# Routed expert blocks advanced one stage at a time, with later constant tables, in a macaron layer on one core

## The chip, the core and the metric

One Trainium2 chip, one core of it. The metric is device time of the whole program in microseconds (us), lower is better; every run's time is that of one launch. The core's engines are named as in the profile: PE (TensorE, matrix products and transpositions), DVE (VectorE), ACT (ScalarE), POOL (GpSimd) and SP (SyncE, which here only issues transfers).

## The reference

x has 8 sequences of 256 tokens with 256 features, float32, so 2048 tokens. The layer is a "macaron": half a feed-forward block, attention, half a feed-forward block, each behind a layer norm.

```
x = x + 0.5 * ffn(layernorm(x))
x = x + attention(layernorm(x))
x = x + 0.5 * ffn(layernorm(x))

ffn(x):                                  # E = 8 experts, K = 2, H = 176
    scores = softmax(x @ gate_w)
    topk_w, topk_idx = top_k(scores, 2)
    routed = sum over the 2 chosen experts e of
             topk_w * ((silu(x @ w_gate[e]) * (x @ w_up[e])) @ w_down[e])
    shared = (silu(x @ sw_gate) * (x @ sw_up)) @ sw_down     # width 352
    return routed + shared

attention(x):                            # 16 heads of 128, one key/value head
    an index score I of 16 small heads picks, for every token, 32 earlier tokens;
    softmax attention over those, then @ wo
```

The gate of the experts is not computed for every expert and token: only the two chosen experts' rows matter, and the kernel uses that.

## The kernel before

Tokens lie in 16 tiles of 128 tokens by 256 features, and x stays in on-chip memory all the time. The function `ffn(n, ...)` is called twice, n = 0 ahead of the attention and n = 1 behind it. The order of instructions on each engine is not written out by hand: the Python code is traced, and a scheduler with priorities from the traced order makes one queue for each engine, each worked off in order. A wait in a queue therefore holds up all that stands behind it in that queue.

**Loads and layer norm.** x is loaded in groups of tiles, 0–1, 2–3, 4–7, 8–11 and 12–15 (L102 to L104), by SP's queue, behind it the shared expert's weights (L107 to L115). `expert_loads` (L121) are six loads of the experts' weights into `wall`, 704 KB each: two pairs of gate and up weights and a pair of down weights; `ffn` lets two of them be issued behind each of the first three groups' layer norms. `layernorm` (L214 to L256) works group by group: statistics `st` (L218) and `mv` (L219) on DVE, `ve` (L221), the square root on ACT, `rstd` (L226), then for each tile `xn` (L248, five buffers), its store to `xn_dram` by SP's queue (L252), its transposition `pt` on PE (L255) and the copy `xnT` on ACT (L256).

**Shared expert.** For each tile `pg` (L455) gives the gate of the shared expert and the router's logits; ACT takes `lg` (L462) and `sg`, the silu (L464). Later `pu` (L472) on PE, `gt` (L480) on DVE, three transpositions `ptg` (L491) on PE, copies `gT` (L492, L494), the product `po` (L498) and the addition to x on DVE (L503). These tiles' work is spread between the other stages.

**Routing.** `route` (L258 to L433) sorts the 4096 pairs of token and expert into blocks of 128 slots that each belong to one expert: 37 blocks (`ND`) are always worked, two more only if the counts ask for them (`rare`, L619). It uses two tables of counts, `place` (128 x 1024) and `block` (128 x 1248), that POOL makes with `iota` (L191, called from L649 and L650).

**Routed blocks.** For block b, POOL gathers its 128 rows from `xn_dram` into `xs` (`fetch`, L511; 8 + 2 buffers); PE transposes them (`px`, L522), ACT copies to `xsT` (L524); PE multiplies with the expert's gate and up weights (`pgu`, L534, `widen`), whose place is read from a table into a register of PE (`locate`); ACT takes the silu `sl` (L544), DVE multiplies to `h` (L546); PE transposes h (`ph`, L562, `turn_hidden`), DVE copies to `hT` (L564); PE multiplies with the down weights (`py`, L570, `narrow`); DVE makes the weight `ws` from two columns that came with the gathered row (L578); ACT scales to `y` (L587) and POOL scatters y to `y_dram` (L589). `routed` (L600 to L616) calls these; its body is quoted here, since the order in it is what the diff rewrites:

```
for b in range(ND):
    h = widen(b)
    if b > 0:
        narrow(b - 1, slot_pool)
    if b + XB < ND:
        fetch(b + XB, slot_pool)
    if b + 2 < ND:
        turn(b + 2)
    turn_hidden(b, h)
narrow(ND - 1, slot_pool)
```

**Behind the loop.** The two result rows of each token are read back by plain transfers (`yg`, L634) and added on DVE (`combine`, L640). In the first call the attention stage follows, in the second the output's store.

Of the kernel before, what the change touches and what calls it, by code (L numbers as in the profile page):

```python
# [23 lines left out]
def macaron_kernel(  # L24
# [42 lines left out]
    SCALE = HD ** -0.5  # L67
    DR = D + 16
    XB = 8
    XH = 2  # L70
    SB = 8
    WAIT = 3
    YB = 1
# [24 lines left out]
    wk_sb = wts.tile([P, KD, HD], F32, name="wk_sb")  # L98
    wv_sb = wts.tile([P, KD, HD + HI], F32, name="wv_sb")

    starts = [0, 2, 4, 8, 12, NT]
    groups = [range(a, b) for a, b in zip(starts, starts[1:])]  # L102
    for g in groups:
        nc.sync.dma_start(out=x[:, g.start : g.stop, :], in_=xr[:, g.start : g.stop, :])  # L104
    nc.scalar.dma_start(out=wsg_sb[:, :, 0:HS], in_=sw_gate.rearrange("(k p) h -> p k h", p=P))
    nc.scalar.dma_start(out=wsg_sb[:, :, HS:], in_=gate_w.rearrange("(k p) e -> p k e", p=P))
# [79 lines left out]
    ones = const.tile([P, P], BF16, name="ones")  # L186
    nc.gpsimd.memset(ones, 1.0)

    def counted(name, pattern, base=0, channel=0, dtype=F32, pool=const):
        t = pool.tile([P] + [n for _, n in pattern], dtype, name=name, bufs=1)  # L190
        nc.gpsimd.iota(  # L191
            t, pattern, base=base, channel_multiplier=channel,
            allow_small_or_imprecise_dtypes=True,
        )
        return t

    expert8 = counted("expert8", [[0, NT], [1, E]], base=-E)
# [236 lines left out]

        return token, dest, choice, cols, used

    def ffn(n, pool, block_pool, behind):

# [2 lines left out]
        xn_dram = dram.tile([NT * P, DR], F32, name=f"xn_dram_{n}")  # L443
        y_dram = dram.tile([(2 * NT * K + NB) * P, D], F32, name=f"y_dram_{n}")
        lg = pool.tile([P, NT, E], F32, tag="lg", name=f"lg_{n}", bufs=1)
        sg = {}
        for tiles in groups:
            layernorm(tiles, xn_dram, table=(n == 0))
            for load in expert_loads[0:2]:
                load()  # L450
            del expert_loads[0:2]
            for i in tiles:
                pg = psum.tile([P, HS + E], F32, tag="A", name=f"pg_{n}_{i}")
                for k in range(KD):
                    nc.tensor.matmul(  # L455
                        pg,
                        xnT[:, k, i * P : (i + 1) * P],
                        wsg_sb[:, k, :],
                        start=(k == 0),
                        stop=(k == KD - 1),  # L460
                    )
                nc.scalar.copy(lg[:, i, :], pg[:, HS:])  # L462
                sg[i] = pool.tile([P, HS], F32, tag=f"sg{i}", name=f"sg_{n}_{i}", bufs=1)
                nc.scalar.activation(sg[i], pg[:, 0:HS], AF.Silu)  # L464

        gts = {}

# [35 lines left out]
            nc.vector.scalar_tensor_tensor(x[:, i, :], po, 0.5, x[:, i, :], ALU.mult, ALU.add)  # L503

        w = wall.rearrange("p e c -> p (e c)")
        xs, xsT, hT, c0 = {}, {}, {}, {}

        def fetch(b, slot_pool):

# [8 lines left out]
        def turn(b):  # L518

            px = psum.tile([P, KD, P], F32, tag="B", name=f"px_{n}_{b}")  # L520
            for k in range(KD):
                nc.tensor.transpose(px[:, k, :], xs[b][:, k * P : (k + 1) * P], ident)  # L522
            xsT[b] = block_pool.tile([P, KD, P], F32, tag="xsT", name=f"xsT_{n}_{b}", bufs=3)
            nc.scalar.copy(xsT[b], px)  # L524

        def locate(b):
# [3 lines left out]
        def widen(b):  # L530

            pgu = psum.tile([P, 2, HE], F32, tag="A", name=f"pgu_{n}_{b}")
            for k in range(KD):
                nc.tensor.matmul(  # L534
                    pgu,
                    xsT[b][:, k, :],
                    w[:, bass.ds(c0[b] + 2 * k * HE, 2 * HE)],
                    start=(k == 0),
                    stop=(k == KD - 1),
                )  # L540
            if b + 1 < ND:
                locate(b + 1)
            sl = block_pool.tile([P, HE], F32, tag="sl", name=f"sl_{n}_{b}", bufs=3)
            nc.scalar.activation(sl, pgu[:, 0, :], AF.Silu)  # L544
            h = block_pool.tile([P, HE], F32, tag="h", name=f"h_{n}_{b}", bufs=3)
            scaled = nc.vector.tensor_tensor(h, sl, pgu[:, 1, :], ALU.mult)  # L546
            if attn_loads:
                load = attn_loads.pop(0)()
                tc.add_manual_dep(
                    load.ins,  # L550
                    scaled.ins.name,
                    mybir.DependencyInfo(
                        mybir.DependencyClass.Sync, mybir.DependencyReason.DATA
                    ),
                    reason="spread over the blocks",
                )
            return h

        def turn_hidden(b, h):
            ph = psum.tile([HH, 2, P], F32, tag="C", name=f"ph_{n}_{b}")  # L560
            for c in range(2):
                nc.tensor.transpose(ph[:, c, :], h[:, c * HH : (c + 1) * HH], ident)  # L562
            hT[b] = block_pool.tile([HH, 2, P], F32, tag="hT", name=f"hT_{n}_{b}", bufs=3)
            nc.vector.tensor_copy(hT[b], ph)  # L564

        def narrow(b, slot_pool):

            py = psum.tile([P, D], F32, tag="D", name=f"py_{n}_{b}")
            for c in range(2):
                nc.tensor.matmul(  # L570
                    py,
                    hT[b][:, c, :],
                    w[0:HH, bass.ds(c0[b] + 2 * KD * HE + c * D, D)],
                    start=(c == 0),
                    stop=(c == 1),
                )
            ws = block_pool.tile([P, 1], F32, tag="ws", name=f"ws_{n}_{b}", bufs=4)
            nc.vector.scalar_tensor_tensor(  # L578
                ws,
                xs[b][:, D + 1 : D + 2],  # L580
                choice[:, b : b + 1],
                xs[b][:, D : D + 1],
                ALU.mult,
                ALU.add,
            )
            y = slot_pool.tile([P, D], F32, tag="y", name=f"y_{n}_{b}", bufs=SB)
            nc.scalar.mul(y, py, ws)  # L587

            stored = nc.gpsimd.indirect_dma_start(  # L589
                out=y_dram,  # L590
                out_offset=bass.IndirectOffsetOnAxis(ap=dest[:, b : b + 1], axis=0),
                in_=y,
                in_offset=None,
            ).ins
            tc.declare_no_dep(stored, group=f"y_{n}", reason="rows that differ")
            tc.add_to_no_dep_group(f"y_{n}", stored)

        def routed(slot_pool):


            for b in range(XB):
                fetch(b, slot_pool)
            locate(0)
            turn(0)
            turn(1)
            for b in range(ND):
                h = widen(b)
                if b > 0:
                    narrow(b - 1, slot_pool)
                if b + XB < ND:  # L610
                    fetch(b + XB, slot_pool)
                if b + 2 < ND:
                    turn(b + 2)
                turn_hidden(b, h)
            narrow(ND - 1, slot_pool)

        def rare(count, slot_pool):

# [25 lines left out]
        def meanwhile(count):  # L644
            for _ in range(count):
                shared(next(tiles))

        with tc.tile_pool(name=f"route{n}", bufs=1, reuse_waits="tile") as tables:
            place = counted(f"place_{n}", [[1, P], [0, NA * K]], dtype=BF16, pool=tables)  # L649
            block = counted(f"block_{n}", [[1, NB], [0, NT * K]], dtype=BF16, pool=tables)  # L650
            token, dest, choice, cols, used = route(n, lg, xn_dram, place, block, tables, pool, meanwhile)
        meanwhile(behind)
        count = nc.values_load(used[0:1, 0:1], min_val=0, max_val=NB)
        with tc.tile_pool(name=f"slots{n}", bufs=1, reuse_waits="tile") as slot_pool:
            routed(slot_pool)
# [222 lines left out]
    with (  # L878
        tc.tile_pool(name="blocks0", bufs=3) as block_pool,
        tc.tile_pool(name="ffn0", bufs=3) as pool,  # L880
    ):
        results, combine, shared, left = ffn(0, pool, block_pool, behind=2)
        for i in left:
            shared(i)

# [69 lines left out]
    with (  # L955
        tc.tile_pool(name="blocks1", bufs=3, reuse_waits="tile") as block_pool,
        tc.tile_pool(name="ffn1", bufs=3, reuse_waits="tile") as pool,
    ):
        results, combine, shared, left = ffn(1, pool, block_pool, behind=2)

        def store(tiles):
            span = slice(tiles[0], tiles[-1] + 1)
            nc.sync.dma_start(out=outr[:, span, :], in_=x[:, span, :])


        late = left[-3:]
        with tc.tile_pool(name="late", bufs=1, reuse_waits="tile") as late_pool:
            for i in left[:-3]:
                shared(i)
            pairs = [range(i, min(i + 2, late[0])) for i in range(0, late[0], 2)]  # L970
            ends = [range(late[0], late[2]), range(late[2], NT)]
            yg = {g: results(g, late_pool, 7) for g in pairs[:4] + ends + pairs[4:]}
            for i in late:
                shared(i, first=lambda: [combine(g, yg[g]) for g in ends if g[0] == i])
                store([i])
            for g in pairs:
                combine(g, yg[g])
                store(g)
# [48 lines left out]
```

## Time and profile before

| | us |
|---|---|
| median of 7 runs | 974.93 (973.3 to 976.77) |
| time of the profiled execution | 974.67 |
| its span in the profile | 972.9 |
| PE busy | 943.5 (97%) |
| DVE busy | 582.6 (60%) |
| ACT busy | 418.5 (43%) |
| POOL busy | 291.1 (30%) |
| mean granted PE clock | 0.998 of full |

The span runs from the first to the last instruction of the profiled execution; the 1.8 us between it and that execution's time lie outside. The profile's page gives the busy time of each engine, and below it the costliest groups of instructions with the idle time ahead of them. Three further views are used below. The timeline lists an engine's instructions in order of start: start, duration, engine, line, operation, output and inputs, how many alike in a row, and in brackets the idle time ahead and what ended it. The waits add up idle time by the pair of what waited and what it waited for. The windows give, for a stretch of time, each engine's busy time, and at the end the granted clock of PE, the busy share of the DMA engines and GB/s. A matmul's duration in these rows is modelled and overlaps with the next one's: the distance from start to start is what it costs in a full queue.

### The profile page before, as it was taken

What the parts mean: (1) busy time and instruction counts of PE and PEld (TensorE: products, weight loads), DVE (VectorE), ACT (ScalarE), POOL (GpSimd) and SP (SyncE); (2) the same over time, 40 slices, a digit from 0 to 9 for tenths busy, and PEclk for the clock granted to TensorE, in tenths of its full rate; (3) what the DMA queues carried; (4) which work ended last, traced back from release to release, by engine and by line L of the source; (5) the groups of instructions that cost most, each with busy time, mean ns of one, the idle gap of its engine ahead of it and who ended that gap; (6) DMA issues with size and microseconds to landing.
All of it is one profiled execution on the core that took longest, in us unless ns stands there. A gap on an engine that the chain in (4) does not pass through costs nothing. (4 is left out here: it accounts for less than half of the span.)

```text
span 972.9 us, 15312 instructions
## 1 busy us (share of the span) xinstructions
PE 943.5 (97%) x4476; PEld 749.7 (77%) x4476; DVE 582.6 (60%) x1642; ACT 418.5 (43%) x1233; POOL 291.1 (30%) x333
## 2 busy tenths in 40 slices
PE   6999999999999999999999999999999989899997
PEld 3677776898888888888888888888877766677765
DVE  5453334986856756766765775585685554633336
ACT  4424443345544535545445444534444434144431
POOL 2037773001312212122221222222133320277740
PEclk9999999999999999999999999999999999999999
DMA  9316632420322222222222222322324330133317
GB/s 307 95 56 191 205 106 93 141 77 22 120 76 87 80 94 67 93 98 77 76 91 96 86 91 74 97 88 75 100 90 132 126 124 24 33 108 107 107 62 264
DMA packets 99576, 100.53 MB, mean 103 GB/s; under 512 B 15942, under 2 KB 82470, under 8 KB 99494
## 3 DMA queue, kind: packets, MB, share of 16 engines
q1 hardware_dynamic: 82502, 51.89, 17.9%
q0 software_dynamic: 14272, 45.18, 13.3%
q10 hardware_dynamic: 2720, 2.47, 0.9%
q8 instruction: 39, 0.64, 0.3%
q14 instruction: 43, 0.35, 0.1%
HBM read 58.07 MB, written 41.42 MB: 102 GB/s over the span
## 5 line engine op out<-in xcount | busy, mean ns | idle before, releaser
L815 POOL TENSOR_TENSOR s<-s,rden 128x512 f32<-128x512 f32 x64 | 93.8, 1466 | 233.0 <-DVE rden L814 128.9
L805 ACT ACTIVATE s<-s,anm 128x128 f32<-128x128 f32 (+1 forms) x256 | 113.0, 443 | 98.4 <-DVE anm L802 49.0
L869 PEld LDWEIGHTS pwo<-wo_sb,oT 128*128 128x128 f32 x512 | 96.4, 190 | 29.6 <-issue 12.0
L869 PE MATMUL pwo<-wo_sb,oT 128*128 128x256 f32 x512 | 117.3, 381 | 0.2 <-ACT oT L848 0.2
L749 DVE SCALAR_TENSOR_TENSOR index<-r,v,index 128x128 f32<-128x128 f32 (+1 forms) x240 | 111.8, 490 | 8.9 <-ACT r L742 7.1
L671 PE MATMUL pqT<-xnT,wq_sb 128*128 128x256 f32 x512 | 116.2, 379 | 0.0
L511 POOL DMA_INDIRECT xs<-xn_dram,token x74 | 71.6, 967 | 128.5 <-DVE dest L416 106.6
L671 PEld LDWEIGHTS pqT<-xnT,wq_sb 128*128 128x128 f32 x512 | 96.9, 190 | 12.4 <-issue 1.0
L671 PE MATMUL pqi<-xnT,wi_sb 128*128 128x224 f32 x512 | 102.8, 352 | 0.0
L534 PE MATMUL pgu<-wall,xsT 128*128 x296 | 100.3, 460 | 0.2 <-ACT xsT L524 0.2
L734 PE MATMUL pi<-kI,qi 128*128 128x128 f32 (+1 forms) x512 | 94.7, 334 | 3.6 <-ACT r L742 3.6
L671 PEld LDWEIGHTS pqi<-xnT,wi_sb 128*128 128x128 f32 x512 | 95.8, 190 | 1.0
L786 PE MATMUL ps<-kT,qT 128*128 128x256 f32 (+1 forms) x512 | 94.6, 327 | 1.7 <-DVE s L793 1.7
L822 DVE STREAM_TRANSPOSE sq<-s 128x512 f32<-128x512 f32 x64 | 62.3, 973 | 54.6 <-POOL s L815 54.6
L841 PE MATMUL pav<-s,v 128*128 128x512 f32 x192 | 93.0, 593 | 1.9 <-DMA s<-sq_dram 1.9
L786 PEld LDWEIGHTS ps<-kT,qT 128*128 128x128 f32 x512 | 81.2, 191 | 17.3 <-ACT r L742 5.1
L734 PEld LDWEIGHTS pi<-kI,qi 128*128 128x128 f32 x512 | 73.7, 191 | 21.0 <-ACT r L742 12.2
L793 DVE TENSOR_TENSOR s<-ps,mb 128x512 f32<-128x512 f32 x96 | 64.2, 681 | 36.8 <-PE ps L786 36.1
L589 POOL DMA_INDIRECT y_dram<-y,dest x74 | 72.2, 975 | 39.2 <-ACT xsT L524 17.5
L742 ACT ACTIVATE r<-pi 128x512 f32<-128x512 f32 x96 | 54.2, 589 | 66.9 <-DVE index L749 51.0
L570 PE MATMUL py<-wall,hT 88*128 x296 | 76.2, 379 | 0.0
L570 PEld LDWEIGHTS py<-wall,hT 88*128 88x128 f32 x296 | 55.9, 189 | 20.4 <-ACT y L587 1.1
(157 smaller groups left out, 1304.4 us busy)
## 6 DMA issues: line engine op xcount, KB each, us to landing
s<-sq_dram SPq DMA_DIRECT2D x384, 64.0 KB, 2.1
sq_dram<-sq POOLq DMA_DIRECT2D x32, 512.0 KB, 2.9
sq_dram<-sq POOLq DMA_DIRECT2D x32, 256.0 KB, 2.5
yg<-y_dram SPq DMA_DIRECT2D x18, 256.0 KB, 2.8
xn_dram<-xn SPq DMA_DIRECT2D x32, 128.0 KB, 1.8
yg<-y_dram SPq DMA_DIRECT2D x7, 512.0 KB, 7.3
wi_sb<-in_L_attn_wq_idx_dram SPq DMA_DIRECT2D x8, 256.0 KB, 3.6
wq_sb<-in_L_attn_wq_dram SPq DMA_DIRECT2D x8, 256.0 KB, 3.6
```

The lines of the kernel that those rows point to most:

```text
L511: nc.gpsimd.indirect_dma_start(out=xs[b], out_offset=None, in_=xn_dram, in_offset=bass.IndirectOffsetOnAxis(ap=token[:, b : b + 1], axis=0),)
L534: nc.tensor.matmul(pgu, xsT[b][:, k, :], w[:, bass.ds(c0[b] + 2 * k * HE, 2 * HE)], start=(k == 0), stop=(k == KD - 1),)
L570: nc.tensor.matmul(py, hT[b][:, c, :], w[0:HH, bass.ds(c0[b] + 2 * KD * HE + c * D, D)], start=(c == 0), stop=(c == 1),)
L589: stored = nc.gpsimd.indirect_dma_start(out=y_dram, out_offset=bass.IndirectOffsetOnAxis(ap=dest[:, b : b + 1], axis=0), in_=y, in_offset= ...
L671: nc.tensor.matmul(ps[:, j, :], weights(k, h0 + hh + j), xnT[:, k, b * S + skip : (b + 1) * S], start=(k == 0), stop=(k == KD - 1),)
L734: nc.tensor.matmul(pl[:, j, :], qi[:, hh + j, t * P : (t + 1) * P], kI[:, 0:ns], start=True, stop=True,)
L749: nc.vector.scalar_tensor_tensor(index[t], r[:, j, :], iw, index[t], ALU.mult, ALU.add)
L786: nc.tensor.matmul(ps[:, j, :], qT[:, j0 + j, t * P : (t + 1) * P], kT[:, 0:ns], start=True, stop=True,)
L805: nc.scalar.activation(s[:, j, :], s[:, j, :], AF.Exp, bias=nm[:, j : j + 1], scale=SCALE, accum_out=den[:, j : j + 1],)
L815: nc.gpsimd.tensor_tensor(s, s, rden.unsqueeze(2).to_broadcast([P, HG, ns]), ALU.mult)
L841: nc.tensor.matmul(po.rearrange("p q h k -> p (q h k)"), v[:, c, 0:HD], pT[:, c].rearrange("p q r -> p (q r)"), start=(c == 0), stop=(c == t),
L869: nc.tensor.matmul(po, oT[:, h, :], wo_sb[:, w0 + h, :], start=(h == 0), stop=(h == HW - 1),)
```

## The change

Four things change, all of them in or around `ffn`.

- The routed loop runs four steps longer and holds one stage of four different blocks in a step: the gate and up products of block b, the gathered rows' transposition of b + 2, the hidden layer's transposition of b − 2 and the down product of b − 4. `fetch` stands last in the step. `xsT`, `h` and `hT` get four buffers instead of three, `xs` thirteen instead of ten.
- `ws` is placed behind the copy `hT` of the same block in DVE's queue.
- In the first call the groups of tiles are 0, 1, 2–3, 4–7, 8–11, 12–15; in the second they stay as they were. The loads of x follow the first list. As two expert loads are issued behind each of the first three groups, they come behind the layer norms of tile 0, of tile 1 and of tiles 2–3.
- The iotas of `place` and `block` wait for the silu of tile 8 (`gate[NT // 2]`).

`behind` becomes the name of a helper that makes one instruction wait for another; what was the parameter `behind` is `ahead` now.

```diff
-    XH = 2
+    XH = 5
...
-    starts = [0, 2, 4, 8, 12, NT]
-    groups = [range(a, b) for a, b in zip(starts, starts[1:])]
-    for g in groups:
+    def grouped(*starts):
+        return [range(a, b) for a, b in zip(starts, (*starts[1:], NT))]
+
+    groups = [grouped(0, 1, 2, 4, 8, 12), grouped(0, 2, 4, 8, 12)]
+    for g in groups[0]:
         nc.sync.dma_start(out=x[:, g.start : g.stop, :], in_=xr[:, g.start : g.stop, :])
...
+    def behind(ins, other, reason):
+
+        tc.add_manual_dep(
+            ins.ins,
+            other.ins.name,
+            mybir.DependencyInfo(mybir.DependencyClass.Sync, mybir.DependencyReason.DATA),
+            reason=reason,
+        )
+
-    def counted(name, pattern, base=0, channel=0, dtype=F32, pool=const):
+    def counted(name, pattern, base=0, channel=0, dtype=F32, pool=const, after=None):
...
+        if after is not None:
+            behind(made, after, "not while VectorE is in a hurry")
...
-        for tiles in groups:
+        for tiles in groups[n]:
...
-                nc.scalar.activation(sg[i], pg[:, 0:HS], AF.Silu)
+                gate[i] = nc.scalar.activation(sg[i], pg[:, 0:HS], AF.Silu)
...
-            nc.vector.tensor_copy(hT[b], ph)
+            turned[b] = nc.vector.tensor_copy(hT[b], ph)
...
-            nc.vector.scalar_tensor_tensor(
-                ws,
...
+            with tc.issue_after(turned[b].ins):
+                nc.vector.scalar_tensor_tensor(
+                    ws,
...
-            for b in range(ND):
-                h = widen(b)
-                if b > 0:
-                    narrow(b - 1, slot_pool)
+            h = {}
+            for b in range(ND + 4):
+                if b < ND:
+                    h[b] = widen(b)
+                if b + 2 < ND:
+                    turn(b + 2)
+                if 2 <= b < ND + 2:
+                    turn_hidden(b - 2, h[b - 2])
+                if b >= 4:
+                    narrow(b - 4, slot_pool)
                 if b + XB < ND:
                     fetch(b + XB, slot_pool)
-                if b + 2 < ND:
-                    turn(b + 2)
-                turn_hidden(b, h)
-            narrow(ND - 1, slot_pool)
...
-            place = counted(f"place_{n}", [[1, P], [0, NA * K]], dtype=BF16, pool=tables)
-            block = counted(f"block_{n}", [[1, NB], [0, NT * K]], dtype=BF16, pool=tables)
+            late = dict(dtype=BF16, pool=tables, after=gate[NT // 2])
+            place = counted(f"place_{n}", [[1, P], [0, NA * K]], **late)
+            block = counted(f"block_{n}", [[1, NB], [0, NT * K]], **late)
```

More of the change, by code (lines that the diff above doesn't have):

```diff
@@ L187, in macaron_kernel @@
     nc.gpsimd.memset(ones, 1.0)
-    def counted(name, pattern, base=0, channel=0, dtype=F32, pool=const):
+    def behind(ins, other, reason):
[6 more added lines that the diff above has]
+    def counted(name, pattern, base=0, channel=0, dtype=F32, pool=const, after=None):
         t = pool.tile([P] + [n for _, n in pattern], dtype, name=name, bufs=1)
-        nc.gpsimd.iota(
+        made = nc.gpsimd.iota(
             t, pattern, base=base, channel_multiplier=channel,
@@ L435, in route, with ffn @@
         return token, dest, choice, cols, used
-    def ffn(n, pool, block_pool, behind):
+    def ffn(n, pool, block_pool, ahead):
         xn_dram = dram.tile([NT * P, DR], F32, name=f"xn_dram_{n}")
@@ L445, in ffn @@
         lg = pool.tile([P, NT, E], F32, tag="lg", name=f"lg_{n}", bufs=1)
-        sg = {}
-        for tiles in groups:
+        sg, gate = {}, {}
+        for tiles in groups[n]:
             layernorm(tiles, xn_dram, table=(n == 0))
@@ L505, in ffn @@
         w = wall.rearrange("p e c -> p (e c)")
-        xs, xsT, hT, c0 = {}, {}, {}, {}
+        xs, xsT, hT, turned, c0 = {}, {}, {}, {}, {}
         def fetch(b, slot_pool):
@@ L522, in turn @@
                 nc.tensor.transpose(px[:, k, :], xs[b][:, k * P : (k + 1) * P], ident)
-            xsT[b] = block_pool.tile([P, KD, P], F32, tag="xsT", name=f"xsT_{n}_{b}", bufs=3)
+            xsT[b] = block_pool.tile([P, KD, P], F32, tag="xsT", name=f"xsT_{n}_{b}", bufs=4)
             nc.scalar.copy(xsT[b], px)
@@ L544, in widen @@
             nc.scalar.activation(sl, pgu[:, 0, :], AF.Silu)
-            h = block_pool.tile([P, HE], F32, tag="h", name=f"h_{n}_{b}", bufs=3)
+            h = block_pool.tile([P, HE], F32, tag="h", name=f"h_{n}_{b}", bufs=4)
             scaled = nc.vector.tensor_tensor(h, sl, pgu[:, 1, :], ALU.mult)
             if attn_loads:
[L548 to L556, printed above, removed]
+                behind(attn_loads.pop(0)(), scaled, "spread over the blocks")
             return h
@@ L562, in turn_hidden @@
                 nc.tensor.transpose(ph[:, c, :], h[:, c * HH : (c + 1) * HH], ident)
-            hT[b] = block_pool.tile([HH, 2, P], F32, tag="hT", name=f"hT_{n}_{b}", bufs=3)
-            nc.vector.tensor_copy(hT[b], ph)
+            hT[b] = block_pool.tile([HH, 2, P], F32, tag="hT", name=f"hT_{n}_{b}", bufs=4)
+            turned[b] = nc.vector.tensor_copy(hT[b], ph)
         def narrow(b, slot_pool):
@@ L577, in narrow @@
             ws = block_pool.tile([P, 1], F32, tag="ws", name=f"ws_{n}_{b}", bufs=4)
-            nc.vector.scalar_tensor_tensor(
-                ws,
[L580 to L585, printed above, removed]
+            with tc.issue_after(turned[b].ins):
+                nc.vector.scalar_tensor_tensor(
+                    ws,
+                    xs[b][:, D + 1 : D + 2],
+                    choice[:, b : b + 1],
+                    xs[b][:, D : D + 1],
+                    ALU.mult,
+                    ALU.add,
+                )
             y = slot_pool.tile([P, D], F32, tag="y", name=f"y_{n}_{b}", bufs=SB)
@@ L648, in ffn @@
         with tc.tile_pool(name=f"route{n}", bufs=1, reuse_waits="tile") as tables:
-            place = counted(f"place_{n}", [[1, P], [0, NA * K]], dtype=BF16, pool=tables)
-            block = counted(f"block_{n}", [[1, NB], [0, NT * K]], dtype=BF16, pool=tables)
+            late = dict(dtype=BF16, pool=tables, after=gate[NT // 2])
+            place = counted(f"place_{n}", [[1, P], [0, NA * K]], **late)
+            block = counted(f"block_{n}", [[1, NB], [0, NT * K]], **late)
             token, dest, choice, cols, used = route(n, lg, xn_dram, place, block, tables, pool, meanwhile)
-        meanwhile(behind)
+        meanwhile(ahead)
         count = nc.values_load(used[0:1, 0:1], min_val=0, max_val=NB)
@@ L881, in macaron_kernel @@
     ):
-        results, combine, shared, left = ffn(0, pool, block_pool, behind=2)
+        results, combine, shared, left = ffn(0, pool, block_pool, ahead=2)
         for i in left:
@@ L958, in macaron_kernel @@
     ):
-        results, combine, shared, left = ffn(1, pool, block_pool, behind=2)
+        results, combine, shared, left = ffn(1, pool, block_pool, ahead=2)
         def store(tiles):
```

## The prediction

> **What bounds the kernel now.** I read the page's busy row first, then TensorE's waits, then the stages around the change in the timeline.
>
> ```profile
> PE 943.5 (97%) x4476; PEld 749.7 (77%) x4476; DVE 582.6 (60%) x1642; ACT 418.5 (43%) x1233; POOL 291.1 (30%) x333
> ...
> PE pt L255 <- DVE xn L248: 9.0, 1, 9.0
> ...
> PE ptg L491 <- DVE gt L480: 2.8, 2, 2.4
> ```
>
> TensorE (PE) is busy 943.5 of 972.9 us, so the path that sets the end is PE's own queue, and a change pays only through PE's waits. The other lines are waits (total, times, longest), the two large ones that the change can touch: 9.0 us before the first transposition, and 2.4 us where ptg waits for VectorE's (DVE) gt.
>
> Next, the stage that gives the change its name. The first line is a window of 25 us in the middle of the first routed loop (PE, PE weight loads, DVE, ACT, POOL, granted clock, DMA share); the others are one step of PE.
>
> ```profile
> 100.00:125.00 25.00, 25.00 (x122) 19.20 (x121) 8.98 (x31) 10.54 (x30) 19.12 (x20) 1.00 0.63 193
> ...
> 101.45 0.38 PE L522 MATMUL px<-ident,xs 128*128 128x128 f32 x2
> 101.67 0.38 PE L562 MATMUL ph<-ident,h 128*88 128x128 f32 x2
> 101.89 1.35 PE L534 MATMUL pgu<-wall,xsT 128*128 x4
> 103.07 1.03 PE L570 MATMUL py<-wall,hT 88*128 x4
> ```
>
> PE is busy 25.00 of 25.00 at clock 1.00. From px to px (101.45 to 103.94, the next px) a step takes 2.49 us, start to start .22 + .22 + 1.18 + .87.
>
> **The change part by part, against the profiled execution: 974.67 us, of which 972.9 is the span.** The median shown is 974.93, .26 above it; I keep to 974.67.
>
> *Routed loop.* The built kernel has the same instructions on PE; a step becomes px(b+2), ph(b-2), py(b-4), pgu(b+1) instead of px(b+2), ph(b), pgu(b+1), py(b). Nothing is removed, and there is no idle time in the step to remove, so I take 0 for the 74 steps. Bounds: a weight load that is now exposed or hidden by the new neighbours, ±.03 us a step, ±2 in all (the reason for .03 is under the second rival). At both ends of the loops: in the first loop's fill PE has gaps of .24, .24 and .34; with two steps in which nothing waits for h they shrink to about .6 together, −.2. In the drain the last three py stand together (py_34, 35, 36): PE takes .86 for each, while POOL takes .98 and a gap of .30 for each scatter, 1.28. So the last scatter is .4 later than PE's last py: +.4 for each loop as far as the combination behind waits for it (bounds −.3 and +1.5 for both); I take +.4 in all, since PE has other tiles' work there. The xs buffers (10 to 13) put 16 gathers ahead of the first scatter instead of 14; POOL is behind PE in steady state already (2.56 us for a gather and a scatter with gaps, against 2.49), and this lead covers 37 × .07 = 2.6 us.
>
> *ws behind hT (L578).* Before the second loop, DVE's queue holds ws_0 and ws_1, which wait for gathers, ahead of gt of tile 8. DVE's and PE's timelines there:
>
> ```profile
> 846.78 0.22 DVE L578 SCALAR_TENSOR_TENSOR ws<-xs,choice 128x1 f32<-128x1 f32 x1 [1.26 <-DMA xs<-xn_dram,token]
> 847.96 0.22 DVE L578 SCALAR_TENSOR_TENSOR ws<-xs,choice 128x1 f32<-128x1 f32 x1 [0.96 <-DMA xs<-xn_dram,token]
> 848.09 0.52 DVE L480 TENSOR_TENSOR gt<-sg,pu 128x352 f32<-128x352 f32 x1
> ...
> 844.89 1.35 PE L472 MATMUL pu<-wsu_sb,xnT 128*128 128x352 f32 x4
> 848.66 0.55 PE L491 MATMUL ptg<-ident,gt 128*128 128x128 f32 x3 [2.43 <-DVE gt L480]
> ...
> 850.18 2.77 PE L498 MATMUL po<-wsd_sb,gT 128*128 128x256 f32 x6
> 852.74 1.43 PE L534 MATMUL pgu<-wall,xsT 128*128 x4
> ...
> 851.00:852.00 1.00, 1.00 (x4) 0.79 (x3) 0.00 (x0) 1.00 (x1) 0.69 (x2) 0.50 0.31 87
> ```
>
> pu ends at 846.23 and could release gt at once; gt runs at 848.09, PE idles 2.43, and then the granted clock is .50 (last line) until it is 1.00 again from 853: six po take 2.77 us, where twelve took 2.76 at 39.7. After the change gt stands first: it begins at about 846.25, takes .52, and PE waits about .6, then .5 for the gathers of px_0 and px_1, which land when they did. At full clock pgu_0 then starts at about 849.57 instead of 852.74: −3.2. With the gaps behind it that wait for h and xsT (.54 and .08) gone too, **−3.8** for this stage; about 1.8 of it is the half clock (3.5 us at half pace before 853). Bounds: −2 (if the waits of 1.1 us still lower the clock; waits of 1.07 and 1.69 elsewhere did not) and −4.3.
>
> *The start.* x comes as tile 0, tile 1, tiles 2–3. Now it is two at a time, and DVE, POOL and SP show:
>
> ```profile
> 5.98 1.31 DVE L221 TENSOR_SCALAR ve<-mv 128x2 f32<-128x2 f32 x1
> ...
> 5.92 1.34 POOL L191 IOTA block<- 128x1248 bf16 x1
> ...
> 15.57 3.83 SPq L252 DMA_DIRECT2D xn_dram<-xn  x4
> 19.45 1.96 SPq L121 DMA_DIRECT2D wall<-in_L_ffn_w_down_dram  x2
> 21.50 12.41 SPq L252 DMA_DIRECT2D xn_dram<-xn  x8
> ...
> 32.18 1.22 DVE L248 TENSOR_SCALAR xn<-x,mv,rstd 128x256 f32<-128x256 f32 x3 [7.34 <-DMA xn_dram<-xn]
> ```
>
> ve of two elements lasts 1.31 us, beside the iota and ending with it: it takes .17 elsewhere. With the iotas later this is gone. In the built queue rstd of the first tiles still stands behind the statistics of tiles 2 and 3, whose x landed at 5.6; eight short DVE operations behind that give xn_0 at about 6.85 and PE's start at **7.35 instead of 9.05: −1.7** (bounds −2.5 and −1).
>
> That lead then meets the stores of xn. xn has five buffers, so xn_9 waits until xn_4's store has landed. Before, SP issues the two w_down loads between xn_7 and xn_8 (lines 3 to 5); PE has then twelve tiles ready, and the wait of 7.34 (last line, xn_13 behind xn_8's store, landed at 32.05) costs PE nothing: pt_13 starts at 32.66, just in time. After, the groups are shorter, and w_down stands ahead of **xn_4's** store. The DMA engines are 98% busy from 0 to 25 us, so order decides: xn_4 lands four stores of about .42 earlier than xn_8 did, 32.05 − 1.7 = 30.4. The moved iotas, behind tile 8's silu, lie at about 27.7 to 31.0 and can hold xn as they held ve, so pt_9 comes at about 31.1. PE's work ahead of it (nine pt at .22, nine pg at 1.24, four pu at 1.2, 18.0 in all, 2.1 lost at half clock as now, where the first eight pg records last 4.18 us and the next eight 2.58, .8 waiting for xn_2's store at pt_7) ends at 7.35 + 18.0 + 2.1 + .8 = 28.2. So PE idles .8 + 2.9 = **+3.7** (bounds 0, if the stores overtake, and +5, if xn_4 lands at 31.7 or so).
>
> An idle time of 2.9 us is longer than the 2.43 that cost half the clock above, so I add the same **+1.8** (bounds 0 and 1.8).
>
> The Trainium skill ("TensorE: Matmul & The Clock Gate", the table of clock states in Part 1) says that the clock falls after at least one idle window of about 3.4 us. The row above had .50 after 2.43 us already, so the row counts; by the rule neither idle time would lower the clock, and without the 1.8 added here the sum would be 973.6.
>
> The rest of the first ffn: pu_3 is earlier, gT_0 and the route's counts wait a little for ACT and POOL: +.5 (bounds −.5 and +1). In the second ffn the iotas lie at 788.5 to 791.8 now and held xn, but PE's wait then was for another transfer issued earlier; moved to about 809 they meet an idle DVE: 0.
>
> **Sum:** −1.7 + 3.7 + 1.8 + .5 (start) − .2 + .4 (loop ends) − 3.8 (second fill) + 0 (steps) = +.7: **975.4 us**.
>
> **The rivals.**
>
> *Faster: PE is not starved at pt_9.* If the DMA engines let xn_4's store by, or SP gets to it before the queue is full, the wait and the half clock behind it go: 975.4 − 3.7 − 1.8 = 969.9; if only the clock stays up, 973.6. For it: most xn stores of the page land in 1.8 us (median). Against: xn_8, behind w_down, took 10.6. It decides if xn_4 lands before 28.
>
> *Slower: the new step order exposes a weight load.* py now follows the two short transpositions directly. A weight load's row is .19, longer than the .11 of one transposition's matmul, so the load for py(b-4) has less cover than the one for py(b) had behind pgu's 1.18. Against: today pgu stands in that place and the step has no gap. A price of .05 to .1 a step (a quarter to half of a load) gives 74 × .05 = +3.7 to +7.4, that is 979.1 to 982.8; it decides from a step of 2.52 us (+2.2), 977.6.
>
> *The change does not do what it says.* The stages two blocks apart have no stall to fill: the step stays 2.49, and all the difference is in the first 35 us and around 846. This is part of my forecast.
>
> **How the numbers follow.** About .2%, 1.95 us, is what a measurement of this kernel can tell from no change. Forecast, 975.4 with its own range 973 to 977.5: .42 (.34 within, .06 slower, .02 faster). Not starved, 969.9 to 973.6: .33 (.28 faster, .05 within). Exposed load, 977.6 and more: .25 (.21 slower, .04 within). Together .30, .43, .27. The range goes from 969.9 to 979.1, which leaves out the far half of the slower case and a little below.
>
> **What would show it.** Right: first pt near 7.35; a wait of 2 to 3 us at pt_9 for xn, ended by a store's landing near 30.4, and .50 behind it; ptg near 846.9 with no half clock; steps of 2.49. Wrong: pt_9 without a wait (first rival), a step above 2.52 with idle PE or longer spacing of py (second), or ptg still over 2 us late because gt waits for something else.

## The result and the profile after

The changed kernel takes 976.28 us (median of 24 runs, 973.91 to 977.92), the kernel before 974.60 (62 runs, 973.12 to 976.97). The ratio is 1.0014, with a 95% interval of 1.0009 to 1.0020: slower by about 1.4 us (the medians alone differ by 1.7). The profiled execution took 975.39 us with a span of 973.7, .7 and .8 above the one of before.

The page's busy row of the changed kernel, then two of PE's waits (total, times, longest):

```profile
PE 941.8 (97%) x4476; PEld 749.1 (77%) x4476; DVE 573.1 (59%) x1644; ACT 418.3 (43%) x1234; POOL 290.4 (30%) x333
```

```profile
PE pt L268 <- DVE xn L261: 11.9, 4, 8.7
...
PE ptg L504 <- DVE gt L493: 2.2, 4, 0.6
```

The one wait of 9.0 for xn became four with 11.9 in all. The two waits for gt, 2.8 in all with one of 2.4, became four of at most .6, 2.2 in all; one of the new ones is in the first call, behind its first px. Line numbers are up to 13 higher in this kernel (pt L268, pg L468, ph L567, py L575).

The routed loop in its steady state, as a window and as one step of PE:

```profile
100.00:125.00 25.00, 25.00 (x123) 19.18 (x122) 7.95 (x30) 10.54 (x30) 19.04 (x20) 1.00 0.65 200
```

```profile
99.98 0.38 PE L535 MATMUL px<-ident,xs 128*128 128x128 f32 x2
100.20 0.38 PE L567 MATMUL ph<-ident,h 128*88 128x128 f32 x2
100.42 1.03 PE L575 MATMUL py<-wall,hT 88*128 x4
101.28 1.35 PE L547 MATMUL pgu<-wall,xsT 128*128 x4
```

The order is the new one, and the next px starts at 102.47: 2.49 us, as before. py directly behind the two transpositions costs nothing.

The start is where the time went. PE's timeline of the changed kernel, the lines with idle time in brackets:

```profile
8.67 1.08 PE L268 MATMUL pt<-ident,xn 128*128 128x128 f32 x4 [8.67 <-DVE xn L261]
...
16.10 2.69 PE L468 MATMUL pg<-wsg_sb,xnT 128*128 128x360 f32 x8 [0.95 <-ACT xnT L269]
...
24.41 0.44 PE L268 MATMUL pt<-ident,xn 128*128 128x128 f32 x2 [0.53 <-DVE xn L261]
...
32.18 0.44 PE L268 MATMUL pt<-ident,xn 128*128 128x128 f32 x2 [1.60 <-DVE xn L261]
33.67 0.41 PE L268 MATMUL pt<-ident,xn 128*128 128x128 f32 x2 [1.05 <-DVE xn L261]
...
38.82 0.44 PE L268 MATMUL pt<-ident,xn 128*128 128x128 f32 x2 [0.45 <-ACT xnT L269]
...
60.15 4.54 PE L403 MATMUL tk<-parts,at 128*128 128x78 bf16 x32
```

What these wait for, in DVE's, SP's and POOL's timelines:

```profile
31.36 3.44 DVE L261 TENSOR_SCALAR xn<-x,mv,rstd 128x256 f32<-128x256 f32 x6 [6.61 <-DMA xn_dram<-xn]
```

```profile
16.30 2.51 SPq L265 DMA_DIRECT2D xn_dram<-xn  x2
18.87 1.33 SPq L123 DMA_DIRECT2D wall<-in_L_ffn_w_down_dram  x2
20.29 16.33 SPq L265 DMA_DIRECT2D xn_dram<-xn  x12
```

```profile
30.04 1.94 POOL L202 IOTA place<- 128x1024 bf16 x1 [25.84 <-ACT sg L477]
31.93 1.45 POOL L202 IOTA block<- 128x1248 bf16 x1
```

xn_9 waits 6.61 us for the store of xn_4, which SP issues behind both w_down loads; it lands at 31.34. The iotas run beside xn_9 and those behind it: six xn take 3.44 us where six of .41 would take 2.5. Waits of 4.58 us in all stand between 9 and 45 us, 3.18 of them for xn and 1.40 for xnT; the timeline of before lists none there. The last line of PE's fence is a row of 32 routing products (`tk`) without a wait, and yet the granted clock falls there (the column ahead of the last two):

```profile
63.00:64.00 1.00, 1.00 (x10) 1.00 (x9) 0.10 (x1) 0.00 (x0) 0.00 (x0) 0.58 0.07 16
64.00:65.00 1.00, 1.00 (x9) 0.99 (x7) 0.24 (x1) 0.00 (x0) 0.00 (x0) 0.50 0.00 0
```

It is below 1.00 from about 63.2 to 66.6, which costs 1.7 us.

The fill of the second call's loop is where the time came from:

```profile
849.62 1.35 PE L485 MATMUL pu<-wsu_sb,xnT 128*128 128x352 f32 x4
851.58 0.55 PE L504 MATMUL ptg<-ident,gt 128*128 128x128 f32 x3 [0.61 <-DVE gt L493]
...
853.02 1.46 PE L511 MATMUL po<-wsd_sb,gT 128*128 128x256 f32 x6
```

The wait is .61, six po take 1.46 instead of 2.77, and the clock stays at 1.00 (the trace's only fall ahead of the end is the one at 63.2).

A ledger at landmarks of PE, after minus before. The first ptg behind the first loop: +4.40 (166.87 against 162.47), the start with the first loop. The attention's first pqT: +4.80 (226.01 against 221.21), so what lies behind the first loop cost .40. The last pg of the second call: +4.71, the attention changes nothing. Its pgu_0: +1.59, the fill gained 3.12. The first ptg behind the second loop: +.78, the loop gained .81. The end of PE's last po: +1.28, what lies behind the second loop cost .50. The span: +.8, since the output's stores end .5 sooner behind PE.

### The profile page after: what moved, and what is told of

Its sections match the earlier page's. It is cut to its first block, busy times and chain, and to the rows that moved or that the text cites. A ratio compares the mean times of both kernels' runs of the same rounds, so it can differ in the third digit from the quotient of the medians.

```text
span 973.7 us, 15381 instructions
## 1 busy us (share of the span) xinstructions
PE 941.8 (97%) x4476; PEld 749.1 (77%) x4476; DVE 573.1 (59%) x1644; ACT 418.3 (43%) x1234; POOL 290.4 (30%) x333
## 4 chain that ended last, share of the span: by engine, by line
PE 75%; DVE 8%; DMA 7%; issue 3%; ACT 3%; POOL 2%; SPq 1%; DVEq 0%; POOLq 0%; ACTq 0%
PE pqT L680 9%; PE pqi L680 9%; PE pwo L878 8%; PE pgu L547 7%; PE pi L743 7%; PE pav L850 7%; PE ps L795 7%; PE py L575 4%; PE po L511 4%; PE pg L468 3%; DMA y_dram<-y,dest 3%; PE pu L485 2%; ACT s L814 2%; DMA s<-sq_dram 1%; PE px L535 1%
## 5 line engine op out<-in xcount | busy, mean ns | idle before, releaser
L559 DVE TENSOR_TENSOR h<-sl,pgu 128x176 f32<-128x176 f32 x74 | 24.9, 337 | 114.0 <-ACT sl L557 114.0
L575 PE MATMUL py<-wall,hT 88*128 x296 | 75.5, 379 | 0.0
```

What stands on the lines that cost most here:

```text
L575: nc.tensor.matmul(py, hT[b][:, c, :], w[0:HH, bass.ds(c0[b] + 2 * KD * HE + c * D, D)], start=(c == 0), stop=(c == 1),)
```

## Experiments

The runs were made on three chips, each beside the kernel before, and the ratios are to that kernel on the same chip: 974.53 us for old_groups, wdown_later, ws_only and no_ws, 974.44 for loop_ws_2, loop_only, late_loads and iota_early_2, and 1019.89 for wdown_act, iota_early, loop_ws and wdown_iota6. That last chip runs every kernel some 40 us longer. Of its runs only the ratios among themselves and the part of their traces ahead of the routed loop are used, and observations on the chip and its clock at the end.

### The groups as they were: old_groups

```diff
-    groups = [grouped(0, 1, 2, 4, 8, 12), grouped(0, 2, 4, 8, 12)]
+    groups = [grouped(0, 2, 4, 8, 12), grouped(0, 2, 4, 8, 12)]
```

> The changed kernel, with the first call's groups of tiles as they were (0-1, 2-3, 4-7, 8-11, 12-15), so that the w_down loads stand again between the stores of xn_7 and xn_8; all else as changed. Theory S (the new start starves PE): in the changed kernel's trace PE idles .95, .53, 1.60, 1.05 and .45 us ahead of 39 us, and the granted clock falls to .50 behind 32 tk matmuls that stand in one row (63 to 66.5, 1.7 us lost); all of it comes from the groups. Then about 5 us go: 971 (970 to 972), with no wait of over .3 us between 9 and 45 us, and tk in pieces at full clock. Theory L (the loop's new order costs, the start is as good as before): 976.

Measured: 971.31 us, ratio .9968 (.9956 to .9980). The waits for xn between 9 and 45 us shrink to one of 1.07 at tile 13, whose xn waits for the store of xn_8 until 32.85, when the iotas (28.6 to 31.8) are over. The clock stays up at the tk products. The new start costs 4.5 us by the ratios (5.0 by the medians) of what the rest of the change gains; theory L falls.

### w_down behind tile 7's store: wdown_later

```diff
-            for load in expert_loads[0:2]:
+            now = 2 * (n == 1 or tiles.start > 0)
+            for load in expert_loads[0:now]:
                 load()
-            del expert_loads[0:2]
+            del expert_loads[0:now]
```

> The changed kernel with its new groups, but no expert loads behind tile 0's layer norm: the three pairs are issued behind tile 1, tiles 2-3 and tiles 4-7, so w_down stands behind xn_7's store again. Theory S, if the cause is the place of w_down ahead of xn_4's store and not the groups themselves: the waits at tiles 9 to 13 go, PE's start stays near 8.7 or comes a little earlier, tk stands in pieces again and the clock stays at 1.00: 970.5 (969.5 to 972). If small groups themselves cost (more short instructions, later x of tiles 2-3): 973 to 975. Theory L: 976.

Measured: 970.16, ratio .9960 (.9947 to .9974). PE starts at 7.57, and one wait of .56 is left. So the small groups are no loss by themselves (.9960 against .9968 with the old ones, with intervals that overlap). The loss is the place of the expert loads, which moved with the groups because they are dealt out two to a group; the trace has w_down ahead of the store that PE waits for.

### ws behind hT alone: ws_only

```diff
+            with tc.issue_after(turned[b].ins):
                 nc.vector.scalar_tensor_tensor(
                     ws,
```

> The kernel before with one thing changed: ws of a block is placed behind its hT copy on DVE. Old loop order, old buffers, old groups, early iotas. Theory S says that the gain in the second call's fill (PE idle 2.43 to .61 us, no half clock behind it) is the ws order's alone: 974.6 - 3.3 = 971.3 (970.8 to 972). Theory L's rival reading, that it is the loop order (no h to wait for in the fill) that gives the gain: 974 to 974.6.

Measured: 972.77, ratio .9982 (.9973 to .9991), a gain of 1.8 instead of 3.3. In its trace the second fill is as expected (wait of .61, no half clock; from the first pgu_0 to the second, at 69.50 and 852.30, 782.80 us, before 785.48: 2.7 less). But in the profiled execution, one of the two slowest of its eleven (974.24), a stretch of half clock lies at 59.8 to 63.2, at the end of the routing products, where the kernel before has none. From the last pg of the second call to its pgu_0 PE takes 29.90 us here, as in the changed kernel, against 33.02 before: the gain there is the order's. That the median gains less has a likely reason in the clock of the kernel before, under "Why the prediction was right" below.

### The change without the order of ws: no_ws

```diff
-            with tc.issue_after(turned[b].ins):
+            if True:
```

> The changed kernel without the placing of ws behind hT; in its queue ws_0 to ws_2 stand ahead of gt of tile 8 in both calls (in the kernel before, in the second call alone). Theory S: the second call's fill loses about 3 us again, the first call's about as much, by a wait of 2 to 3 us at ptg and a half clock behind it: 979 to 982. If the new loop order hides these waits: 976 to 977.

Measured: 981.10, ratio 1.0069 (1.0055 to 1.0083), as theory S had it. PE waits 2.73 for gt in the first call and 2.46 in the second, each with half clock behind it; the last pg to pgu_0 takes 32.57 us again. Its start also shows what the changed kernel's did not: the wait at tile 9 in one piece. PE's timeline and the windows behind it:

```profile
32.18 0.82 PE L268 MATMUL pt<-ident,xn 128*128 128x128 f32 x4 [2.91 <-DVE xn L261]
```

```profile
33.00:34.00 1.00, 0.92 (x2) 0.66 (x3) 0.41 (x2) 0.40 (x2) 0.00 (x0) 0.50 0.76 252
34.00:35.00 1.00, 1.00 (x5) 0.63 (x4) 0.52 (x2) 0.00 (x0) 0.00 (x0) 0.50 0.81 270
```

After 2.91 us of idle time the clock is .50 for 3.4 us; after 1.60 and 1.05 with a pt between them, in the changed kernel, it stayed at 1.00.

### w_down on ACT's queue: wdown_act

```diff
             w_down[:, c * HH : (c + 1) * HH, :].rearrange("e h d -> h e d"),
+            queue=nc.scalar,
...
+                if n == 0 and tiles.start == 2:
+                    with tc.issue_after(gate[1].ins):
+                        load()
```

> The changed kernel, groups and all, but the two w_down loads go out on ACT's queue (behind the copies of tiles 2 and 3, about 15 us) instead of SP's, so that no store of xn stands behind them in its own queue; the bytes are the same. Theory Q (the stores are late because they stand behind w_down in one queue): xn_4's store lands before 27 instead of at 31.3, PE's waits of 1.60 and 1.05 at tiles 9 and 10 go, and the time is about 972 with the clock's drop at the tk row (that row is in one piece here too) or 971 without. Theory B (the DMA engines are full, whatever the queue): xn_4 lands at 29 to 31 still and the time stays at 975 to 976.

Measured on the slower chip: 1019.53, where the changed kernel with early iotas took 1014.96. The changed kernel itself was not run there, so the time decides nothing, and the trace has to. Theory Q fails; theory B had the landing of xn_4 about right, but neither foresaw the wait that came. PE's and DVE's timelines:

```profile
28.45 0.66 PE L269 MATMUL pt<-ident,xn 128*128 128x128 f32 x2 [5.41 <-DVE xn L262]
```

```profile
27.89 0.41 DVE L262 TENSOR_SCALAR xn<-x,mv,rstd 128x256 f32<-128x256 f32 x1 [7.41 <-DMA xn_dram<-xn]
```

Now PE waits 5.41 us at tile 7, for the store of xn_2. That store stands in SP's queue behind the second pair of gate and up weights, and w_down from ACT's queue is under way beside them. xn_4's store lands at 29.3, two us sooner than in the changed kernel, but xn_2's lands at 27.9 instead of 23.9. The edit also issues w_down earlier, at 14.3 and 14.9 us instead of 18.9 and 19.4, so the run shows that the delay moved to another store, not how much of that is the second queue's.

### The iotas early: iota_early and iota_early_2

```diff
-            late = dict(dtype=BF16, pool=tables, after=gate[NT // 2])
+            late = dict(dtype=BF16, pool=tables)
```

> The changed kernel with the iotas of place and block not held back (they run from 4 to 7 us again). Theory S: they hold up xn_9 and xn_10 by about .9 in the changed kernel (iota 30.0 to 33.4 beside xn at 31.4 to 34.8) and cost .4 at the start when early, since tile 0's and 1's statistics wait for x of tiles 2-3 (6.8) anyway: 975.5 (974.5 to 976). Theory I (the iotas matter, DVE is in a hurry at the start): 977 or more, with PE's first pt at 10 or later.

> The changed kernel with early iotas once more, beside the kernel before on another chip than the first time. In its first trace PE's first pt came at 7.9 and PE waited 2.58 at tile 9, so the place of the iotas moved the end of the layer norm's products by nothing (44.41 against 44.33). Theory S: 975.5 to 976.5, as the changed kernel, ratio 1.001 to 1.002. Theory I (late iotas pay): 977 or more.

Measured: 1014.96 on the slower chip (.9946 of the kernel before there), and 973.74 for iota_early_2, ratio .9999 (.9990 to 1.0008). Both expectations of the second run are missed, on the good side: by the ratios, .9999 against 1.0014, early iotas are some 1.5 us better than late ones in this kernel. Its PE timeline has the wait at tile 9, and none behind it at tile 10:

```profile
30.71 0.89 PE L268 MATMUL pt<-ident,xn 128*128 128x128 f32 x4 [1.65 <-DVE xn L261]
```

PE starts at 7.91 with the iotas at 4 to 7 us (8.67 with late ones). At the start they cost at most .3: from the statistics of tiles 2-3 to xn_0 DVE takes 1.57 us (5.78 to 7.35), against 1.27 in wdown_later with late ones. In this kernel xn_9 and xn_10 take .41 each, where the late iotas stretched them to .76 and 1.48; so the wait of 1.05 at tile 10 is the late iotas'.

### The loop's order with and without ws: loop_ws, loop_ws_2, loop_only

The diffs are those of the change; loop_ws leaves groups and iotas as before, loop_only also leaves out issue_after. loop_ws_2 is loop_ws once more.

> Loop order, buffers and ws order as changed; groups and iotas as in the kernel before (nothing of the start is changed). Beside the run with the old groups (971.3, whose iotas were late) and the run with the ws order alone (972.8). Theory S: the start is that of the kernel before (first pt at 9.05, no wait of 1.07 at tile 13), so 970.7 (970 to 971.5); the loop order adds about 1 us for each call in the loop's fill and drain and gives some .5 back behind it. If the loop order gives nothing: 972.8.

> Loop order, buffers and ws order as changed, start as before; the kernel run already on the chip where everything took 45 us longer (0.9897 of the kernel before there), once more to have it beside the kernel before on another. Theory S: PE has no idle time in the loop to fill, so the loop order is worth 1 to 2 us over the ws order alone: 970.8 (970 to 971.7), ratio .996. Theory D (the deeper pipeline is worth as much wherever it runs): ratio .990, 965.

> The loop's new order and buffers alone; ws is not placed behind hT (in the second call ws_0 and ws_1 stand ahead of gt of tile 8 again), start as before. Theory S: PE's wait of 2.4 us for gt in the second fill stays, with the half clock behind it, and the loop order gives 1 to 2 us in the fills and drains: 973.2 (972.5 to 974) where the kernel before takes 974.6, ratio .9985. If the loop order carries the whole gain: 971; if it is worth nothing: 974.6.

Measured: loop_ws 1010.62, ratio .9897 (.9877 to .9918) on the slower chip; loop_ws_2 970.42, ratio .9968 (.9959 to .9978); loop_only 973.33, ratio .9994 (.9985 to 1.0003). The second is as theory S expected; the third agrees with its time, but its interval takes in 1, so by itself the loop order can't be told from no change. From pgu_0 to the first ptg behind the loop, loop_ws_2 takes 94.14 and 94.10 us in the two calls, the kernel before 95.21 and 94.96: 1.07 and .86 less. loop_only takes 94.14 and 93.78 there, ws_only 95.58 and 95.00, so this gain is the loop order's. The steps are as long as before; it is the fill (before, .34 and .20 of waits of ph for h) and the drain, where before each ph starts about .09 late and py_36 waits for its hT. Behind the loops some is given back: from that ptg to the first pqT .42, in the second call from it to PE's end .60.

### The iotas behind tile 6: wdown_iota6

```diff
-            late = dict(dtype=BF16, pool=tables, after=gate[NT // 2])
+            late = dict(dtype=BF16, pool=tables, after=gate[6])
```

This is wdown_later with one edit.

> The kernel with three pairs of expert loads behind tile 1, tiles 2-3 and tiles 4-7 (970.2), with the iotas behind the silu of tile 6 instead of tile 8, when DVE has nothing to do. Theory S: the iotas then run from about 24 to 27 and no longer beside the xn that waits for its buffer at 32, so the .56 at tile 13 goes: 969.6 (969.2 to 970.2). If that wait is the store's alone: 970.2.

Measured on the slower chip: 1008.70, ratio .9891 (.9866 to .9916), which can't be set beside wdown_later's time. In its trace the iotas run from 24.7 to 28.0, and the wait at tile 13 is still there, .70: it is the store's. Theory S falls here.

### All expert loads later: late_loads

```diff
-            for load in expert_loads[0:2]:
+            now = 2 * (tiles.start >= 4)
+            for load in expert_loads[0:now]:
                 load()
...
-            late = dict(dtype=BF16, pool=tables, after=gate[NT // 2])
+            late = dict(dtype=BF16, pool=tables)
```

> The changed kernel with the three pairs of expert loads behind the layer norms of tiles 4-7, 8-11 and 12-15, so that few of them stand ahead of a store of xn, and with the iotas early. Theory S: PE starts at 7.5 to 8.7 and has no wait of over .3 us for xn, the loads land long before their first use at 67 us: 969.5 (968.5 to 970.3), ratio .9948, the fastest of all. If an xn store still waits behind two loads (704 KB each, about 2 us): waits of about 1 us at tiles 9 to 13 and 970.5.

Measured: 969.72, ratio .9959 (.9946 to .9973), the fastest beside wdown_later's 970.16 and .9960; the two can't be told apart. PE's timeline has two waits ahead of 60 us:

```profile
7.92 1.09 PE L268 MATMUL pt<-ident,xn 128*128 128x128 f32 x4 [7.92 <-DVE xn L261]
...
15.35 2.69 PE L469 MATMUL pg<-wsg_sb,xnT 128*128 128x360 f32 x8 [0.48 <-ACT xnT L269]
```

It beats both kernels, the one before by .41% and, by the ratios, the changed one by .55%, with the change's loop, ws order and groups kept.

## Why the prediction was right, and where it was not

It forecast +.7 us on the profiled execution; that was +.7, and +1.4 by the ratio; the median of 976.28 lies .9 above the 975.4 and inside the range. The order of events was as forecast (a gain in the second fill, a loss to starvation at the start), but several terms were off and made up for each other. By its own steps:

- **Routed steps, 0:** right, 2.49 us in both. Second rival: the exposed load does not show.
- **Second fill, −3.8:** up to pgu_0 −3.12, forecast −3.2. The wait of .61 and the full clock were as forecast. From the last pg to pgu_0 the kernels with ws behind hT take 29.90 (changed, ws_only), those without it 33.02 (before), 33.05 (loop_only) and 32.57 (no_ws): ws ahead of gt is the cause. The gaps of .6 behind pgu_0 are part of the second loop's −.81, which is the loop order's. What the forecast missed is that the half clock is not lost in every execution of the kernel before: of its 41 executions listed beside old_groups and late_loads, 11 have a mean clock of 1.000 (972.65 to 974.46 us) and 30 have less (973.72 to 975.58). So about 1.7 of the gain is there in some executions only.
- **PE's start, −1.7:** only −.38. The failing part is the landing of tiles 2-3's x, taken at 5.6 us from before: DVE went on with it at 6.84. In seven other traces with these groups that was 5.72 to 6.28, and PE started between 7.55 and 8.11, so the term is −.4 to −1.5. Late iotas were part of it, but with early ones and these groups PE starts at 7.91 to 7.94.
- **Starvation, +3.7:** 3.18 for xn (.53 at tile 7, 1.60 at tile 9, 1.05 at tile 10), and 1.40 for xnT that was not forecast. The store at which PE waits, and why, are as forecast (xn_4 landed at 31.34, forecast 30.4); old_groups, wdown_later and late_loads take it away by the place of the loads. The iotas' share was counted as .6 of it; with them early the waits behind PE's start are 2.5 instead of 4.6.
- **Half clock behind it, +1.8:** not there in the profiled execution, since the wait fell into 1.60 and 1.05. A half clock of 1.7 us came instead at the routing products, which was not forecast. The sum was saved by an accident here.
- **Rest of the first ffn, +.5:** no run has it alone. Start, waits and the fall at the products come to some +5.8, the ledger stands at +4.40 behind the first loop, and the loop order gains 1.07 there; that leaves about −.4, an estimate.
- **Loop ends, −.2 and +.4:** the loop order gains about 1 us a call from pgu_0 to the first ptg behind the loop, and .40 and .50 are given back behind it. The gain in the drains was missed; in the first call it is hidden in the start's sum.
- **First rival (not starved):** it did not happen in the change, but its price was right in sum: 969.9 was its figure, and 970.16 and 969.72 are what the kernels without starvation take. In part that is luck too, since the 1.8 of half clock in it stands for a fall at another place.

What stays open: how often an execution loses the clock. Of the changed kernel's 26 executions whose clock is listed, the 5 at 1.000 take 973.9 to 974.7, the 11 at .996 or less 975.4 to 977.9; one stretch of 3.4 us at half pace is .0017 of the mean clock, so those have two or more. The 1.4 us by which the change is slower is no more than one such stretch costs. Between executions without any, at 1.000, the medians are 974.1 (5) and, for the kernel before, 973.2 (11). The last section shows what decides in the traces; for the executions without a trace it is not shown.

The Trainium skill ("TensorE: Matmul & The Clock Gate", the table of clock states in Part 1) names one idle window of about 3.4 us. The traces here agree with the length, 3.41 us, but PE need not be idle throughout: waits of 2.39 (loop_only), 2.43, 2.46, 2.73 and 2.91 us were each followed by 3.41 us at .50. No length of a wait alone decides either: one of 1.79 in loop_ws was followed by a fall, one of 2.33 in the same trace was not.

## What to carry to other kernels

When a loop over groups also deals out loads, a change of the groups moves the loads past other transfers of the same queue; read the queue's order before the engines'. A buffer that is freed by a store's landing makes a full DMA queue a wait of PE: put what is needed last, last. A second queue did not help in wdown_act; another store was late instead. In an in-order queue, place a small instruction that waits for a late transfer behind the work that something else waits for.

## What the runs showed of the hardware

In each of the 14 traces the granted clock changes only at points that lie whole multiples of 3.41 us apart (in the changed kernel 11.96, 63.16 and 66.57; in the kernel before 13.22, 849.48 and 852.89). Where these points fall against the program differs from trace to trace. What PE did in the 3.41 us ahead of such a point goes with what the clock does behind it:

| trace and point | PE idle in the 3.41 us ahead | routing products in them | clock behind |
|---|---|---|---|
| before, 849.48 | 2.57 | 0 | .50 |
| no_ws, 32.88 | 2.71 | 0 | .50 |
| loop_ws, 102.72 | 1.88 | 0 | .50 |
| loop_ws, 942.40 (the wait of 2.33, cut in two by a point) | 1.86 | 0 | 1.00 |
| changed kernel, 32.44 (the wait of 1.60) | 1.60 | 0 | 1.00 |
| changed kernel, 63.16 | 0 | 3.00 | .50 |
| ws_only, 59.82 | 0 | 2.80 | .50 |
| no_ws, 63.60 | 0 | 2.63 | 1.00 |
| iota_early_2, 63.49 | 0 | 2.23 | 1.00 |

Over all traces, from full clock, it fell behind all 20 stretches with 1.88 us or more of idle time, behind 4 of 8 with 1.70 to 1.86, and with less only behind the 3 that hold 2.80 us or more of routing products (the third is wdown_act's, at 66.85). These products (bf16, 78 columns, each with a weight load; a row of 32 takes 4.54 us) show PE as busy without a gap, so a busy share of 1.00 in the timeline does not keep the clock up. It follows, though no run tests it, that the same wait or the same row can cost 1.7 us in one execution and nothing in the next, by where the points fall.

On one chip the same kernels took 40 to 45 us longer, nearly all of it in the two routed loops (loop_ws: from pgu_0 to the end of the last py 109.9 and 112.2 us; loop_ws_2: 91.9 and 91.8). There PE, DVE and ACT stand nearly idle together for 1 to 5 us at a time. A line of PE's timeline and a window from loop_ws:

```profile
78.92 2.71 PE L547 MATMUL pgu<-wall,xsT 128*128 x4 [4.29 <-issue]
```

```profile
75.00:76.00 1.00, 0.00 (x0) 0.00 (x0) 0.00 (x0) 0.00 (x0) 0.69 (x2) 1.00 0.39 96
```

The trace names no releaser for these waits ("issue" is none), and the cause is open. The loop order's deeper pipeline and the ws order gained 1% there (.9897) against .3% elsewhere (.9968). That the stages two blocks apart bridge these stalls would fit, but it is not shown: neither order was run alone on that chip.
